# A three-stage token-mixing kernel: the first sequence's chain on two engines, another order at the mixer's beginning, and residuals loaded with the last chunk

## The chip, the cores and the metric

The kernel runs on one core of one Trainium2 chip. The core has a matrix engine (TensorE, PE in the profile), three engines for elementwise work (VectorE or DVE, ScalarE or ACT, GpSimd or POOL), and a SyncE queue (SP) that issues transfers; transfers run on 16 DMA engines. In this kernel matmuls read tiles in SBUF and write tiles in PSUM, from where DVE or ACT take them on. The metric is the device time of one execution in microseconds, as the median of several runs.

## The reference

The input x has 8 sequences of 1024 tokens with 128 channels (an image of 32 by 32). Two layers are computed, all in float32. Cut to what matters here:

```python
x = x + attention(group_norm(x))            # 4 heads of 32, q and k scaled to length 1, softmax over 1024 tokens
t = to_tokens(x)
t = t + mamba(layer_norm(t), forward weights) + reversed(mamba(reversed(layer_norm(t)), backward weights))
t = t + spectral_filter(layer_norm(t))      # 16 long filters over the sequence, by a Fourier transform
return t
```

In mamba the tokens are projected, a part of the projection passes a causal convolution of four taps per channel and a SiLU, a recurrence over chunks of 64 tokens follows, and its output is gated, normalised and projected back. The spectral filter transforms each sequence, multiplies every frequency by a 128 x 128 matrix and transforms back; the result is added to the residual t.

## The kernel before

One function, `fast_kernel`, holds all stages. In nearly all of them PE, DVE, ACT and POOL run their instructions in the order in which the program writes them (`manual_schedule(engines=IN_ORDER)`); in the mixer SP does too (`ALL_IN_ORDER`). Elsewhere a planner sets SP's order, and in the tail (L1589 to L1632) that of every engine.

**Attention (L591 to L816).** `qkv(b)` is a generator that makes q, k and v of one sequence, in steps divided by `yield`. PE transposes x (L609) into a PSUM tile `pt`. DVE copies it to the SBUF tile `xt` (L611) and takes statistics of `xt` (L615, L617). Two matmuls with one column each sum them over the groups of four channels; DVE works with small tiles between them (L622 to L630), and POOL computes the inverse root (L130, L132, tile names `gn_v` and `gn`). DVE normalises `xt` in place (L633). Then, for q and for k: two matmuls into `pq`, a DVE copy to SBUF (L648), and the squares' sum on ACT (L652). After the squares of q, POOL adds the output bias to x (L654). After those of k, POOL computes the inverse lengths (L656, L658), and DVE scales k by them (L673); between the two v is made (L662, L670). The scores need the scaled k.

`transforms` is another generator. It makes Fourier tables on DVE: for each table, angles (L289), then a rounding (L295, L297) and a clamp (L298); ACT turns them into sines (L302). The driver advances the generators by hand: for the first sequence in ten steps (L764 to L770), with one step of `transforms` behind each of the steps 1, 2, 3, 4, 5 and 7. Two steps of `qkv(1)` follow, and then 128 units of scores. PSUM tiles with the tag "t", the score tiles among them, come from a pool of three. `weighted` turns each half sequence's denominators over (copy, four reciprocals, two reductions, a product with `av`); for the last half this is finished in the mixer's beginning.

**Mixer (L826 to L1406).** Units are pairs of sequence and direction. A unit's steps are functions that the program calls in an order written out by hand:
- `project_x(u, n)` makes one half of the convolution's input on PE (`pp`, L935), `copy_x` copies it to SBUF on ACT (L955), `first_tap` writes one tap with the bias on ACT (L960), and `convolve` adds three taps on DVE (L968). `activate_x` is the SiLU.
- `add_decays` (`pdec`, L864 and L866), `turn_decays` and `take_decays` make tables of decays: small matmuls, ACT copies and exponentials, a store of `cums` to memory, and four loads that spread it over the tiles `lm` and `ec` (L889, L896). `from_row` is POOL's subtraction on `lm` (L912).
- `project_bc` is the matmul group `pb` (L990), `activate_bc` its SiLU (L1006).
- `project(B - 1, 1, ...)` (L427, L429) ends attention: four matmuls on `av` into `last_py`, and a DVE addition to x.

Wide PSUM tiles `w` come from `ps_w`, a pool of two.

**Filter chunks (L1485 to L1587).** 16 chunks of 8 frequencies. `matrices` combines the matrices of the next chunk (L1500) from `mst` into the tile `gs` (two buffers), `apply` multiplies (L1534) with the loaded spectra `u`, and `gather` sums (L1549 to L1555) and stores to `yd` (L1557). `fetch` reads the first part of `yd` back into `early_yt` (L1565).

**Tail (L1589 to L1632).** Four pieces (k, h): block of tokens and half of the sequences. `loaded` reads the piece's rows of `yd` into `yt` (two loads of 1 MB; the first piece has `early_yt`) and the residual from `xa` into `res` (1 MB). Three pieces are loaded ahead. `back` combines on DVE (`z`, L1608), transforms back on PE (`pz`, L1613), scales and adds to `res` on DVE (L1620), and stores 1 MB from ACT's queue (L1623).

Of the kernel before, what the change touches and what calls it, by code (L numbers as in the profile page):

```python
# [8 lines left out]
F32 = mybir.dt.float32  # L9
# [5 lines left out]
P = 128  # L15
B = 8
# [29 lines left out]
def fast_kernel(ctx: ExitStack, tc: tile.TileContext, a: dict, out: bass.AP, bad: bass.AP):  # L46
# [544 lines left out]
    with ExitStack() as s:  # L591
# [11 lines left out]

        def qkv(b):
# [6 lines left out]
            nc.vector.tensor_copy(xt, pt)  # L611
            yield
            st = p2.tile([P, 2, 6], F32, tag="st", name=f"st{b}")
            for i in range(2):
                nc.vector.bn_stats(st[:, i, :], xt[:, i * 512 : (i + 1) * 512])  # L615
# [21 lines left out]
            for i, (name, dst) in enumerate((("q", qs), ("k", ks))):  # L637
# [14 lines left out]
                nc.scalar.activation(junk, to, AF.Square, accum_out=ss[:, i : i + 1])  # L652
                if i == 0:
                    nc.gpsimd.tensor_tensor(xin, xin, bout.unsqueeze(1).to_broadcast([P, NT, C]), ALU.add)  # L654
                    yield
# [15 lines left out]
            vs.append(v)  # L671
            yield
# [91 lines left out]
        for at in range(10):  # L764
            next(coming)
            if at in (1, 2, 3, 4, 5, 7):
                next(making)
            if at == 4:
                sines(inv)
        next(coming, None)  # L770
        coming = qkv(1)
# [54 lines left out]
    with ExitStack() as s:  # L826
# [400 lines left out]
        def take_x(u, n):  # L1227
            project_x(u, n)
            copy_x(u, n)
            first_tap(u, n)  # L1230

# [13 lines left out]

        add_decays(first)
        turn_decays(first)
        take_decays(first)
        for _ in ending:
            pass  # L1250
        for n in range(2):
            take_x(first, n)
        add_decays(units[1])
        convolve(first, 0)
        activate_x(first, 0)
        project(B - 1, 1, av, wide_psum(ps_w, "last_py")[:, :512].rearrange("p (i c) -> p i c", i=4))
# [157 lines left out]
    with ExitStack() as s:  # L1414
        mp = s.enter_context(tc.tile_pool(name="c_m", bufs=1, side="right"))
        mst = mp.tile([P, 32, C], F32, name="mst")
# [68 lines left out]
        with ExitStack() as s2:  # L1485
# [103 lines left out]
        with ExitStack() as s2:  # L1589
            p2 = s2.enter_context(tc.tile_pool(name="i_2", bufs=2))  # L1590
            p3 = s2.enter_context(tc.tile_pool(name="i_3", bufs=3))
            ps_o = s2.enter_context(tc.tile_pool(name="i_ps_o", bufs=4, space=PSUM))

            def loaded(k, h):

                yt = early_yt
                if k or h:
                    yt = p2.tile([P, 2, 4, 4, C], F32, tag="yt", name=f"yt{k}_{h}")
                    for i in range(2):
                        nc.sync.dma_start(yt[:, i], yd[:, k, h * 4 : h * 4 + 4, i])  # L1600
                res = p3.tile([P, 4, 4, C], F32, tag="res", name=f"res{k}_{h}")
                nc.sync.dma_start(res, xa[h * 4 : h * 4 + 4, :, NB - 1 - k].rearrange("b p r c -> p b (r c)"))
                return yt, res

            def back(k, h, yt, res):
                z = p2.tile([P, 2, 2, 4, C], F32, tag="z", name=f"z{k}_{h}")
# [3 lines left out]
                for r in (0, 2, 1, 3):  # L1610
                    po = ps_o.tile([P, 4, C], F32, tag="o", name=f"pz{k}_{h}_{r}")
                    for i in range(2):
                        nc.tensor.matmul(  # L1613
                            po,
                            lhsT=inv[:, r, i, :],
                            rhs=z[:, r // 2, i] if r % 2 else yt[:, i, :, r // 2, :],
                            start=(i == 0),
                            stop=(i == 1),
                        )
                    nc.vector.scalar_tensor_tensor(  # L1620
                        res[:, :, r, :], po, keep[:, blk : blk + 1], res[:, :, r, :], ALU.mult, ALU.add
                    )
# [816 lines left out]
```

## Time and profile before

| What | us |
|---|---|
| median of 3 runs (lowest, highest) | 1432.75 (1431.81, 1436.02) |
| the profiled execution: its own time | 1432.01 |
| its span, first to last instruction | 1430.2 |
| 0 to 30: to the first scores, PE busy | 12.99 of 30.0 |
| 30 to 455.6: attention, PE busy | 418.29 of 425.6 |
| 455.6 to 481.6: the mixer's beginning, PE busy | 17.83 of 26.0 |
| 481.6 to 1026.9: mixer, PE busy | 513.83 of 545.3 |
| 1026.9 to 1116: filter, transforms, PE busy | 77.49 of 89.1 |
| 1116 to 1381.4: filter chunks, PE busy | 263.40 of 265.4 |
| 1381.4 to 1430.2: tail, PE busy | 30.89 of 48.8 |

Over the whole span PE is busy for 1334.7 us, DVE 1095.4, ACT 914.5 and POOL 529.5. In a timeline a line has the start, the duration, the engine, the line of the kernel, the operation, output and inputs, and in brackets the idle time of the engine before it and what ended that. "xN" joins N instructions in a row. A matmul of this kernel appears as two instructions. Busy time of PE includes modelled ends.

### The profile page before, as it was taken

Reading aid. Unit: us, or ns where it says so; the run is one execution under the profiler, and the core shown is the slowest. Engines: PE = TensorE matmul, PEld = TensorE weight load, DVE = VectorE, ACT = ScalarE, POOL = GpSimd, SP = SyncE. Lnnn points to the kernel's source line nnn. Section 1 sums busy time; section 2 is a strip of 40 time slices with the busy share of each in tenths; the row PEclk is TensorE's granted clock in tenths of the full one; section 3 lists DMA queues with packets and bytes.
Section 4 is the critical chain, followed back from the end, with each engine's and each line's share of the span. In section 5 each row is a group of like instructions: output and inputs, shape, how many; then the busy total and the mean of one; then the engine's idle time right before and its main releaser. Section 6 shows DMA issues by size and latency. Waiting matters only on the chain. (4 is left out here: it accounts for less than half of the span.)

```text
span 1430.2 us, 45285 instructions
## 1 busy us (share of the span) xinstructions
PE 1334.7 (93%) x19782; PEld 839.8 (59%) x19782; DVE 1095.4 (77%) x2138; ACT 914.5 (64%) x1421; POOL 529.5 (37%) x510
## 2 busy tenths in 40 slices
PE   5999999999998899999999999998799899999977
PEld 2323333233333566666666666666689899999963
DVE  5779888788768588979787988889644677777745
ACT  3665666766757678778787878786454555555520
POOL 3327866875610243324242424233476111111100
PEclk9999999999999899999999999999999999999989
DMA  7100111110000433434343444442459232222258
GB/s 182 40 1 21 55 38 38 38 51 25 8 1 19 102 76 79 100 90 105 75 105 88 94 92 114 95 106 46 132 190 232 73 89 76 71 77 70 72 153 324
DMA packets 139382, 123.09 MB, mean 86 GB/s; under 512 B 44808, under 2 KB 118152, under 8 KB 135080
## 3 DMA queue, kind: packets, MB, share of 16 engines
q1 hardware_dynamic: 137064, 115.93, 31.6%
q8 instruction: 157, 2.57, 0.8%
q10 hardware_dynamic: 2112, 4.19, 0.8%
q14 instruction: 49, 0.40, 0.1%
HBM read 78.15 MB, written 34.08 MB: 78 GB/s over the span
## 5 line engine op out<-in xcount | busy, mean ns | idle before, releaser
L696 ACT ACTIVATE pr<-pt 128x1024 f32<-128x1024 f32 x256 | 248.1, 1021 | 115.1 <-PE pt L691 113.5
L721 DVE TENSOR_TENSOR two<-pr,pr 128x1024 f32<-128x1024 f32 x128 | 162.9, 1313 | 20.5 <-ACT pr L696 19.6
L1513 ACT COPY gs<-pg 128x512 f32<-128x512 f32 x256 | 132.6, 602 | 64.4 <-PE pg L1500 47.9
L1511 DVE COPY gs<-pg 128x512 f32<-128x512 f32 x256 | 158.7, 682 | 15.3 <-PE pg L1500 9.6
L691 PE MATMUL pt<-q,k 32*128 32x512 f32 x1024 | 159.8, 654 | 7.0 <-ACT pr L696 4.7
L1500 PE MATMUL pg<-taps,mst 32*128 32x128 f32 x4096 | 146.0, 281 | 4.9 <-ACT gs L1513 4.1
L1500 PEld LDWEIGHTS pg<-taps,mst 32*128 32x128 f32 x4096 | 134.0, 189 | 17.1 <-issue 11.6
L712 PE MATMUL po<-pr,v 128*32 128x512 f32 x1024 | 139.9, 605 | 0.0
L926 POOL TENSOR_TENSOR ec<-ec,ct 128x2048 f32<-128x2048 f32 x16 | 83.4, 5212 | 135.3 <-ACT cums L868 59.2
L990 PE MATMUL pb<-bxt,wbc 128*128 128x512 f32 x256 | 116.9, 610 | 13.9 <-ACT zs L981 11.3
L1534 PE MATMUL py<-gs,u 128*32 128x128 f32 (+1 forms) x4096 | 127.8, 277 | 0.0
L968 DVE SCALAR_TENSOR_TENSOR xs<-xp,cw,xs 128x1024 f32<-128x1024 f32 x96 | 121.8, 1281 | 3.5 <-issue 1.7
L1534 PEld LDWEIGHTS py<-gs,u 128*32 128x32 f32 (+1 forms) x4096 | 112.0, 140 | 7.2
L1523 POOL TENSOR_SCALAR u<-u 128x512 f32<-128x512 f32 x16 | 24.0, 1498 | 229.3 <-PE pg L1500 128.5
L691 PEld LDWEIGHTS pt<-q,k 32*128 32x128 f32 x1024 | 47.6, 186 | 85.0 <-issue 32.2
L990 PEld LDWEIGHTS pb<-bxt,wbc 128*128 128x128 f32 x256 | 48.2, 193 | 73.1 <-issue 55.6
L1087 DVE SCALAR_TENSOR_TENSOR state<-state,dec,pst 128x64 f32<-128x64 f32 x448 | 87.3, 274 | 1.1
L1196 POOL TENSOR_TENSOR rms<-rms_v,mhalf 128x8 f32<-128x8 f32 x16 | 27.2, 1698 | 161.2 <-DVE rms_v L1194 161.2
L712 PEld LDWEIGHTS po<-pr,v 128*32 128x32 f32 x1024 | 27.8, 109 | 88.5 <-issue 84.6
L912 POOL TENSOR_TENSOR lm<-cs,lm 128x2048 f32<-128x2048 f32 x16 | 57.9, 3621 | 50.2 <-DVE xs L968 33.8
L732 PE MATMUL pd<-two,ones 128*32 128x512 f32 x512 | 73.0, 613 | 0.2
L1166 PEld LDWEIGHTS spo<-wo,y 128*128 128x128 f32 x512 | 62.1, 191 | 15.3 <-issue 10.3
(280 smaller groups left out, 2763.8 us busy)
## 6 DMA issues: line engine op xcount, KB each, us to landing
lm<-cd SPq DMA_DIRECT2D x32, 512.0 KB
ec<-cd SPq DMA_DIRECT2D x32, 512.0 KB
ud<-sp SPq DMA_DIRECT2D x8, 1024.0 KB
u<-ud SPq DMA_DIRECT2D x32, 256.0 KB
yd<-sums SPq DMA_DIRECT2D x32, 256.0 KB
moved<-state SPq DMA_DIRECT2D x48, 128.0 KB
yt<-yd SPq DMA_DIRECT2D x6, 1024.0 KB
X<-in_x SPq DMA_DIRECT2D x8, 512.0 KB
```

The lines of the kernel that those rows point to most:

```text
L691: nc.tensor.matmul(pt[:, i, :], lhsT=k[rows, j * P : (j + 1) * P], rhs=q[rows, cols], start=True, stop=True)
L696: nc.scalar.activation(pr[:, 2 * g : 2 * g + 2, :].rearrange("p i t -> p (i t)"), pt.rearrange("p i t -> p (i t)"), AF.Exp, scale=SCALE,)
L712: nc.tensor.matmul(po[rows, :], lhsT=vs[b][:, j, rows], rhs=pr[:, h, :], start=(j == 0), stop=(j == NT - 1))
L721: nc.vector.tensor_tensor(two, sums["pr"][:, 2 * g : 2 * g + 2, :], pr[:, 2 * g : 2 * g + 2, :], ALU.add)
L926: t = nc.gpsimd.tensor_tensor(u.ec, u.ec, u.ct.unsqueeze(1).to_broadcast([P, NH, NT, L]), ALU.mult)
L968: u.convolved = nc.vector.scalar_tensor_tensor(acc, xp[:, at : at + T], cw[u.d][:, n, i : i + 1], acc, ALU.mult, ALU.add)
L990: nc.tensor.matmul(u.pb[:, i * 512 : (i + 1) * 512], lhsT=wbc[u.d][:, k, :], rhs=xt[:, at : at + 512], start=(k == 0), stop=(k == KC - 1),)
L1087: nc.vector.scalar_tensor_tensor(u.state[:, k, h, :], u.state[:, k - 1, h, :], u.dec[:, c, h, j : j + 1], u.pst[c][:, j, h, :], ALU.mult, ...
L1500: nc.tensor.matmul(pts[g][:, e, :], lhsT=mst[rows, n * 4 + e, :], rhs=taps[rows, cols].rearrange("p f q m i -> p (f q m i)"), start=True, ...
L1511: nc.vector.tensor_copy(to, frm)
L1513: nc.scalar.copy(to, frm)
L1534: nc.tensor.matmul(py[t * 32 : t * 32 + 32 - 16 * m, q // 2, :], lhsT=u[:, i, m:, :, :, q * FC + f].rearrange("p k b i -> p (k b i)"), rhs ...
```

## The change

Three places change.

In attention, for the first sequence only: `xt` is copied by ACT, while DVE takes the statistics from PSUM; the squares are taken from PSUM (`pq`) instead of the SBUF copy; and the bias is added to x after v is made, not between q and k. The steps of `transforms` come later: three behind step 4, one each behind steps 5 and 7, and one after the end of `qkv(0)`.

In the mixer's beginning the first unit's `project_x` and `copy_x` for half 0 come first, then `add_decays`, the rest of `weighted`, and the other half. `turn_decays` and `take_decays` follow after that. `last_py` is made behind one tap of the convolution, and before the second unit's `add_decays`.

In the tail, residuals get two tiles that hold all pieces: `room`, a further buffer of the tag "gs", and a further buffer of the tag "mst". Of 4 MB, 3 MB are requested at the beginning of the last chunk, and 1 MB among the loads of `yt`. These lie in the rest of `room`, so that each piece has its own place. `z` takes buffers of the tag "u", `pz` those of the tag "g". The last piece is worked on in two halves of two sequences, each with its own store. The tail now lies within the block whose engines run in program order.

```diff
 def qkv(b):
...
-            nc.vector.tensor_copy(xt, pt)
+            first = b == 0
+            if first:
+                nc.scalar.copy(xt, pt)
+            else:
+                nc.vector.tensor_copy(xt, pt)
...
-                nc.vector.bn_stats(st[:, i, :], xt[:, i * 512 : (i + 1) * 512])
+                nc.vector.bn_stats(st[:, i, :], (pt if first else xt)[:, i * 512 : (i + 1) * 512])
...
-                nc.scalar.activation(junk, to, AF.Square, accum_out=ss[:, i : i + 1])
+                nc.scalar.activation(junk, pq if first else to, AF.Square, accum_out=ss[:, i : i + 1])
                 if i == 0:
-                    nc.gpsimd.tensor_tensor(xin, xin, bout.unsqueeze(1).to_broadcast([P, NT, C]), ALU.add)
+                    if not first:
+                        add_bias(xin)
                     yield
...
             vs.append(v)
+            if first:
+                add_bias(xin)
             yield
...
             next(coming)
-            if at in (1, 2, 3, 4, 5, 7):
+            for _ in range({4: 3, 5: 1, 7: 1}.get(at, 0)):
                 next(making)
             if at == 4:
                 sines(inv)
         next(coming, None)
+        next(making)
         coming = qkv(1)
...
+        project_x(first, 0)
+        copy_x(first, 0)
         add_decays(first)
+        for _ in ending:
+            pass
+        first_tap(first, 0)
+        project_x(first, 1)
+        copy_x(first, 1)
         turn_decays(first)
         take_decays(first)
-        for _ in ending:
-            pass
-        for n in range(2):
-            take_x(first, n)
+        first_tap(first, 1)
+        convolve(first, 0, range(1))
+        project(B - 1, 1, av, wide_psum(ps_w, "last_py")[:, :512].rearrange("p (i c) -> p i c", i=4))
         add_decays(units[1])
-        convolve(first, 0)
+        convolve(first, 0, range(1, pad))
         activate_x(first, 0)
-        project(B - 1, 1, av, wide_psum(ps_w, "last_py")[:, :512].rearrange("p (i c) -> p i c", i=4))
         convolve(first, 1)
...
+            def load_residuals(k, b, n):
+                nc.sync.dma_start(
+                    res[k][:, b : b + n].rearrange("p b r c -> p b (r c)"),
+                    xa[b : b + n, :, k].rearrange("b p r c -> p b (r c)"),
+                )
...
                 if c + 1 < chunks:
                     gs[c + 1] = p2.tile([P, P, C], F32, tag="gs", name=f"gs{c + 1}")
                     us[c + 1] = loaded_spectra(c + 1)
+                else:
+
+                    room = p2.tile([P, P, C], F32, tag="gs", name="room")
+                    res = [room[:, :32, :], mp.tile([P, 32, C], F32, tag="mst", name="res1")]
+                    res = [t.rearrange("p (b r) c -> p b r c", b=B) for t in res]
+                    load_residuals(1, 0, B)
+                    load_residuals(0, 0, 4)
...
+            for n, (k, h) in enumerate(pieces[1:], 1):
+
+                yts.append(room[:, 32 * n : 32 * n + 32].rearrange("p (i b q) c -> p i b q c", i=2, b=4))
+                for i in range(2):
+                    nc.sync.dma_start(yts[n][:, i], yd[:, k, h * 4 : h * 4 + 4, i])
+                if n == 2:
+                    load_residuals(0, 4, 4)
+            for yt, (k, h) in zip(yts, pieces):
+                z = p2.tile([P, 2, 2, 4, C], F32, tag="u", name=f"z{k}_{h}")
...
+                size = 2 if (k, h) == pieces[-1] else 4
+                for b in range(0, 4, size):
+                    bs = slice(b, b + size)
+                    to = res[blk][:, h * 4 + b : h * 4 + b + size]
+                    for r in (0, 2, 1, 3):
+                        po = ps_g.tile([P, 4, C], F32, tag="g", name=f"pz{k}_{h}_{b}_{r}")[:, :size]
...
+                        nc.vector.scalar_tensor_tensor(
+                            to[:, :, r, :], po, keep[:, blk : blk + 1], to[:, :, r, :], ALU.mult, ALU.add
+                        )
+                    nc.scalar.dma_start(
...
```

More of the change, by code (lines that the diff above doesn't have):

```diff
@@ L602, in fast_kernel, with add_bias @@
         qs, ks, vs = [], [], []
+        def add_bias(xin):
+            nc.gpsimd.tensor_tensor(xin, xin, bout.unsqueeze(1).to_broadcast([P, NT, C]), ALU.add)
         def qkv(b):
@@ L1225, in fast_kernel @@
         first, norms, av = units[0], {}, avs[1]
[L1227 to L1230, printed above, removed]
         def end(u, pool, waiting=None):
@@ L1415, in fast_kernel @@
         mp = s.enter_context(tc.tile_pool(name="c_m", bufs=1, side="right"))
-        mst = mp.tile([P, 32, C], F32, name="mst")
+        mst = mp.tile([P, 32, C], F32, tag="mst", name="mst")
         early_yt = mp.tile([P, 2, 4, 4, C], F32, name="early_yt")
@@ L1587, in fast_kernel @@
             fetch(chunks - 1)
[L1589 to L1606, printed above, removed]
+            pieces = [(k, h) for k in range(NB) for h in range(2)]
+            yts = [early_yt]
+            for n, (k, h) in enumerate(pieces[1:], 1):
[6 more added lines that the diff above has]
+                z = p2.tile([P, 2, 2, 4, C], F32, tag="u", name=f"z{k}_{h}")
                 for r, i, op in ((0, 0, ALU.subtract), (0, 1, ALU.add), (1, 0, ALU.add), (1, 1, ALU.subtract)):
@@ L1609, in back @@
                 blk = NB - 1 - k
[L1610 to L1618, printed above, removed]
-                        )
-                    nc.vector.scalar_tensor_tensor(
-                        res[:, :, r, :], po, keep[:, blk : blk + 1], res[:, :, r, :], ALU.mult, ALU.add
-                    )
@@ L1623, in back @@
-                nc.scalar.dma_start(
-                    out[h * 4 : h * 4 + 4, blk * 512 : (blk + 1) * 512].rearrange("b (p r) c -> p b (r c)", r=4), res
-                )
-            pieces = [(k, h) for k in range(NB) for h in range(2)]
-            got = [loaded(*piece) for piece in pieces[:3]]
-            for n, piece in enumerate(pieces):
-                back(*piece, *got[n])
-                if n + 3 < len(pieces):
-                    got.append(loaded(*pieces[n + 3]))
+                size = 2 if (k, h) == pieces[-1] else 4
@@ new lines, in fast_kernel @@
+                for b in range(0, 4, size):
[3 more added lines that the diff above has]
+                        po = ps_g.tile([P, 4, C], F32, tag="g", name=f"pz{k}_{h}_{b}_{r}")[:, :size]
+                        for i in range(2):
+                            nc.tensor.matmul(
+                                po,
+                                lhsT=inv[:, r, i, :],
+                                rhs=z[:, r // 2, i, bs] if r % 2 else yt[:, i, bs, r // 2, :],
+                                start=(i == 0),
+                                stop=(i == 1),
+                            )
+                        nc.vector.scalar_tensor_tensor(
+                            to[:, :, r, :], po, keep[:, blk : blk + 1], to[:, :, r, :], ALU.mult, ALU.add
+                        )
+                    nc.scalar.dma_start(
+                        out[h * 4 + b : h * 4 + b + size, blk * 512 : (blk + 1) * 512].rearrange(
+                            "b (p r) c -> p b (r c)", r=4
+                        ),
+                        to.rearrange("p b r c -> p b (r c)"),
+                    )
```

## The prediction

> **What bounds the kernel now.** I read the page's slices first, then the chain of waits, then the timelines of the three places that the diff touches, then TensorE's (PE's) granted clock there. From 30 us on PE is the busy engine of every stage: 418.3 of 425.6 us in attention (30 to 455.6), 513.8 of 545.3 in the mixer after its beginning, 263.4 of 265.4 in the filter chunks. The diff changes none of these loops. It works in the seams, where PE waits: 0 to 30 us (busy 13.0 of 30), 455.6 to 481.6 (17.8 of 26) and 1381.4 to the end (30.9 of 48.8). A microsecond taken from the waiting there is one off the end, as all later work hangs on it.
>
> The timeline of the first sequence (start, duration, engine, line; in brackets the idle time before and its releaser):
>
> ```profile
> 7.28 1.22 DVE L611 COPY xnt<-xt 128x1024 f32<-128x1024 f32 x1
> 8.53 1.29 DVE L615 BATCH_NORM_STATS2 st<-xnt 128x6 f32<-128x512 f32 x2
> ...
> 12.58 1.09 POOL L130 TENSOR_SCALAR gn_v<-var 128x1 f32<-128x1 f32 x1 [5.01 <-DVE var L630]
> ...
> 14.76 2.34 POOL L654 TENSOR_TENSOR X<-X,bout 128x1024 f32<-128x1024 f32 x1
> 14.82 2.83 DVE L633 TENSOR_SCALAR xnt<-xnt,mean,gn 128x1024 f32<-128x1024 f32 x1 [0.47 <-POOL gn L132]
> ...
> 25.55 1.06 ACT L652 ACTIVATE junkk<-k 128x1024 f32<-128x1024 f32 x1 [1.60 <-DVE k L648]
> ...
> 28.23 0.81 DVE L673 TENSOR_SCALAR k<-k,inv 128x1024 f32<-128x1024 f32 x1 [0.92 <-POOL inv L658]
> ```
>
> It is one chain on DVE, POOL and PE; PE's first scores start at 29.19, behind L673. See L633: 2.83 us where its median over eight is 0.76, beside the bias add on POOL.
>
> The mixer's beginning, PE and ACT:
>
> ```profile
> 464.27 1.16 PE L427 MATMUL last_py<-wout,av 128*128 128x128 f32 x8 [0.43 <-ACT xp L955]
> 467.99 10.05 PE L990 MATMUL pb<-bxt,wbc 128*128 128x512 f32 x16 [2.57 <-DVE X L429]
> ```
> ```profile
> 478.08 1.38 ACT L1006 ACTIVATE bt<-pb,cb 64x512 f32<-64x512 f32 x2 [5.21 <-PE pb L990]
> ```
>
> PE waits 2.57 us for one DVE addition (it frees pb's PSUM room), which stands behind three taps of 3.92 us; then the same 16 matmuls take 10.05 us that take 7.14 and 7.11 in the next two units. The stretches show why (us; busy time and count of PE, granted clock, DMA share, GB/s):
>
> ```profile
> 463.80:467.20 3.40, 1.20 (x9) 0.98 1.06 224
> 467.30:473.70 6.40, 5.71 (x7) 0.50 0.70 150
> 473.80:478.10 4.30, 4.24 (x10) 0.99 0.00 0
> ```
>
> The tail, from the chain of waits (start, us, what):
>
> ```profile
> 1381.41 0.32 SPq L1557
> ...
> 1381.84 7.56 DMA res<-xa
> ...
> 1389.59 10.04 PE pz L1613 x16
> ...
> 1400.57 9.38 DMA out<-res
> ...
> 1409.97 10.46 DMA res<-xa
> ```
> and from its timeline:
> ```profile
> 1383.65 0.64 SPq L1565 DMA_DIRECT2D early_yt<-yd  x2
> ...
> 1416.65 1.98 PE L1613 MATMUL pz<-yt,inv 128*128 128x512 f32 x4 [1.57 <-DMA yt<-yd]
> ...
> 1423.28 0.38 ACTq L1623 DMA_DIRECT2D out<-res  x1
> ```
>
> PE's first tail matmul needs only early_yt; its last 128 KB are issued at 1383.65 behind a 1 MB residual load and used at 1389.59. From 1390 to 1420 the DMA share is 1.03 to 1.06 at 380 to 410 GB/s: transfers set the tail.
>
> [...] L633 ends 0.55 us after POOL's addition (17.65 against 17.10). [...]
>
> **Start.** (a) The copy of xt goes to ACT, free then (a 1024-wide PSUM copy there: 0.99), and the statistics read PSUM at 7.28 instead of 8.53: 1.25 saved. PSUM reading can cost 0 to 0.1 (two 512-wide DVE copies from PSUM take 0.69 each); I take 0.1. (b) Table work moves behind the normalisation; the copy of the mean waited 0.3 for L289: saved. POOL's pair gn_v, gn took 2.2 beside DVE table work; its shortest instances are 0.19 and 0.58. Bounds 0.8 to 2.2; I take 1.0, so 1.2 saved. (c) L633 without the addition: 0.76, 2.07 saved. It ends 4.7 earlier (1.25-0.1+0.3+1.2+2.07), near 12.9. (d) Behind it DVE now has tables of 3.8 us (0.3+0.88+0.68+1.25+0.69); before, it waited 3.9 for pq there. The copy of q is not late. (e) The square of k reads PSUM when pk is done (6.55 after L633's end; ACT's sines and the square of q are over by 6.3), not after the DVE copy: 1.3 saved, so POOL's pair behind it starts 6.0 earlier. Copy of k, now behind the fwd angles, is 0.4 late but ends before that pair. (f) The bias add now stands directly behind this pair on POOL, as it stood before L633. L673 will be blocked as L633 was: 2.8 for 0.81, 2.0 given back. Bounds 0.8 and 2.9. (g) The last table step (1.22+0.69 on DVE) now stands before qkv(1)'s copy, which frees the third score tile for PE; ACT has exponentials for part of it: 0 to 1.9 lost, I take 1.0. Sum: 6.0-2.0-1.0 = 3.0 (1.0 to 6.0).
>
> **Mixer.** pp0 goes first and needs no POOL table: after pd at 455.6 instead of 459.0. By durations of the profile (pp 1.86 each, pdec group 1.35, ACT copy 1.0, tap 1.24): pp0 to 457.5, pdec to 458.9, pp1 to 460.8, its copy to 461.8. The denominators are ready at 461.7 as before (DVE's queue is unchanged up to there). last_py runs 462.0 to 463.2, the first tap on DVE 461.7 to 463.0, the freeing addition 463.2 to 463.95; pdec of the next unit ends on PE at 464.6; pb starts 464.6, not 467.99: 3.4. The work of PE between 455.6 and 464.6 leaves no gap over 1.3 us, so the clock should stay full and pb take 7.1, not 10.05: 2.9 more (bounds 0 and 2.9). pb's end, 471.7, meets ACT's second silu: DVE's taps end at 470.3 (461.7+six of 1.3+0.7), silu 471.4. The decays' store is issued 2.4 later (after 462.0), so the table lm, whose transfers ran 462 to about 467, lands near 470; POOL's L912 wants it only behind the taps. ACT's decay exponentials, with the second first tap behind them, and SP's five issues, behind which nothing waits, are thus covered; without this cover each us late would count. Sum 6.3 (3.4 to 6.4).
>
> **Tail.** 3 of 4 MB of residuals are to be loaded when the last chunk's matmuls free the two buffers (about 1371 and 1373): at 400 GB/s, 8 us, over near 1381 to 1383, beside 8.97 us of PE work that needs no DMA. On the SP queue, whose order is not written by hand here, the late yd stores and early_yt stand behind them. yd's last store comes at 1381.4 when most is over; early_yt then lands about 1387: PE starts 2.6 earlier (bounds -1 and 3.5). The 1.57 us stall and 0.4 of the 1.30 us wait for the last residual go: 7.4 MB (6.3 yt, 1 residual) need 19 us from 1386, and the last piece starts 24 us later. Last piece in halves: the same PE passes (128-wide ones run at 0.11, so 256-wide should scale), 0.3 lost to z; last addition 0.75 to about 0.42; last store 512 KB instead of 1 MB, whose transfer kept the DMA engines busy from 1424 to 1427: 1.4. One more store on ACT's queue costs nothing, ACT being idle. Sum 2.6+1.6+0.4-0.3+0.3+1.4 = 6.0 (2.4 to 7.5).
>
> **Total.** 3.0+6.3+6.0 = 15.3. The profiled execution took 1432.0 (span 1430.2 and 1.8 around): 1416.7. The median of three is 0.7 higher; I put the forecast between: 1417.0.
>
> **Rivals.**
> 1. Half clock stays for pb: 2.9 less gained, 1419.9. [...] against: PE's density.
> 2. The loads delay the read-back: SP waits in order for a yd store that lies behind 3 MB, PE starts at 1389.6 or later; with 3 less, 1420. For: one queue; against: the load fits into the last chunk.
> 3. L673 is not blocked: 2.0 more, 1415.0. For: DVE's table steps could shift the meeting; against: the same order gave the block at 14.8.
> 4. Slower: attention settles into another rhythm. Place: 128 score units of 3.3 us (425.6/128), three score tiles in turn; (g) shifts DVE against ACT at the first. Price: each 0.1 us per unit costs 12.6 over 126 units; from 0.09 the kernel is no longer measurably faster, and from 0.16 it is slower: (15.3+4.3)/126. At 0.17, 1438. For: ACT idles 115 us before its exponentials; against: orders and durations in the loop are the same, and PE is 98% busy there.
>
> **How the numbers follow.** Forecast 0.45, rival 1 0.17, rival 2 0.19, rival 3 0.12, rival 4 0.07. 0.3% (4.3 us) is about what can be told from no change. All but rival 4 are faster; of its 0.07 I give 0.02 to within 0.3% and 0.05 to slower: 0.93, 0.02, 0.05. The range 1411 to 1423 takes in rivals 1 to 3, the ends of (b), (f), (g) and the tail's bounds; above lie rivals 1 and 2 together and rival 4.
>
> **What would show it.** Right: L673 near 22 us but lasting some 2.8; bt starting 16.2 us after attention's last pd ends, not 22.5; clock 1.0 throughout pb; pz starting 5.6 after the last sums instead of 8.2; no DMA wait among pz. Wrong: gn_v and gn still 2.2; pb at 10; early_yt later than 8 us after the sums; exponentials in attention at another mean spacing.

## The result, and the profile after

The changed kernel takes 1418.7 us (median of four runs, 1414.25 to 1422.47) where the kernel before took 1434.17 beside it (four runs). The ratio is 0.9892, with an interval of 0.9857 to 0.9927: 1.1% less time. A second comparison, with five runs, gave 1418.27 and a ratio of 0.9907 (0.9892 to 0.9923). The prediction was 1417.0.

The profile after was taken in the shortest of the four runs (1414.25, span 1412.4). Its mean granted clock was 0.987; in the three other runs it was 0.978 to 0.981, as in the kernel before (0.978). Some of the difference between the two traces is therefore clock. The table cuts the span at marks that all kernels have. "Again" is the profile of the second comparison, with a clock of 0.979; "best" is the kernel that is put together at the end of the experiments.

| us | before | after | again | best |
|---|---|---|---|---|
| start to the first scores | 29.19 | 26.78 | 26.84 | 22.90 |
| to the end of attention's last pd | 426.41 | 424.49 | 427.15 | 426.63 |
| to the start of the second pb | 45.37 | 38.26 | 38.33 | 38.10 |
| to the end of the last pg | 870.19 | 867.29 | 869.91 | 869.05 |
| the last chunk's py, behind it | 8.93 | 10.61 | 11.81 | 11.81 |
| to the first pz | 9.50 | 7.36 | 7.53 | 7.46 |
| to the end | 40.61 | 37.61 | 37.13 | 38.15 |
| span | 1430.2 | 1412.4 | 1418.7 | 1414.1 |

Against "again", the start gives 2.4 us, the mixer's beginning 7.0, and the tail 2.6 (5.5 less 2.9 in py). The long loops between differ by under 1 us there. In the profile after they are 1.9 and 2.9 us shorter, which goes with its higher clock.

The start of the kernel after, from its timeline (start, duration, engine, line, operation; in brackets the idle time before it and what ended that):

```profile
8.09 1.30 DVE L623 BATCH_NORM_STATS2 st<-xt 128x6 f32<-128x512 f32 x2 [0.73 <-ACT xnt L617]
...
12.79 0.81 DVE L641 TENSOR_SCALAR xnt<-xnt,mean,gn 128x1024 f32<-128x1024 f32 x1 [0.97 <-POOL gn L132]
...
21.54 1.03 ACT L660 ACTIVATE junkk<-pk 128x1024 f32<-128x1024 f32 x1 [1.68 <-DVE k L656]
...
23.75 2.34 POOL L605 TENSOR_TENSOR X<-X,bout 128x1024 f32<-128x1024 f32 x1
...
23.82 2.82 DVE L684 TENSOR_SCALAR k<-k,inv 128x1024 f32<-128x1024 f32 x1 [1.77 <-POOL inv L667]
...
29.69 2.37 PE L702 MATMUL pt<-q,k 32*128 32x512 f32 x8 [0.81 <-DVE xnt L619]
```

See two waits between readers of one PSUM tile. The statistics wait 0.73 us for ACT's copy of the same `pt`. ACT, idle for 1.68 us, takes the square of k only when DVE's copy of the same `pk` is over; that is 1.4 us after the last matmul of `pk` (20.18). The bias addition on POOL now meets the scale of k, which takes 2.82 us as the normalise did before.

The mixer's beginning, from the timeline, and then from the stretches (us; busy time and count of PE, its weight loads, DVE, ACT, POOL; granted clock, DMA share, GB/s):

```profile
457.51 1.13 PE L427 MATMUL last_py<-wout,av 128*128 128x128 f32 x8 [1.01 <-ACT cs L889]
...
459.60 8.81 PE L1002 MATMUL pb<-bxt,wbc 128*128 128x512 f32 x16
...
468.45 1.38 ACT L1018 ACTIVATE bt<-pb,cb 64x512 f32<-64x512 f32 x2 [1.64 <-PE pb L1002]
```
```profile
455.50:459.60 4.10, 3.09 (x20) 1.94 (x18) 3.98 (x6) 3.37 (x8) 0.00 (x0) 1.00 0.04 8
459.60:463.00 3.40, 3.40 (x6) 1.42 (x6) 3.36 (x3) 2.73 (x4) 0.00 (x0) 0.51 0.77 164
463.00:468.40 5.40, 5.40 (x13) 2.09 (x11) 2.99 (x7) 1.06 (x1) 1.51 (x1) 0.99 1.02 215
```

From the end of pd (451.27) to pb there are 8.33 us instead of 12.39, and pb no longer waits for an addition. Here the granted clock was 0.51 for the first 3.4 us of pb, and the group took 8.81 us. In "again" it took 7.12, 1.7 less:

```profile
462.31 7.12 PE L1002 MATMUL pb<-bxt,wbc 128*128 128x512 f32 x16
```

In "again" a half-clock stretch of 6.8 us begins behind pb, at 472.0 (ten matmuls of sx took 2.40 us there, and 16 took 1.97 in the profile after), so that from pd to the second pb it takes 38.3 us in both.

The tail: the timeline of PE first, then the end of the chain of waits (start, us, what).

```profile
1356.76 8.33 PE L1546 MATMUL py<-gs,u 128*32 128x128 f32 x292
1366.30 1.13 PE L1546 MATMUL py<-gs,u 128*32 128x128 f32 x28 [1.22 <-issue]
1374.79 5.20 PE L1637 MATMUL pz<-early_yt,inv 128*128 128x512 f32 x8 [7.35 <-DMA early_yt<-yd]
...
1399.44 0.92 PE L1637 MATMUL pz<-room,inv 128*128 128x256 f32 x3 [1.85 <-DMA room<-yd]
```
```profile
1356.83 8.26 PE py L1546 x289
1368.73 2.39 DMA yd<-sums
1374.29 2.93 SPq L1580
1377.26 2.70 SPq L1621
1380.00 19.39 DMA room<-yd
1399.44 6.80 PE pz L1637 x30
```

The read-back is earlier, as wanted, but PE now stands idle inside the last chunk for 1.22 us, put down to "issue", that is, to nothing that the profile shows. Before, the chunk's matmuls ran without a gap:

```profile
1371.09 9.00 PE L1534 MATMUL py<-gs,u 128*32 128x128 f32 x320
```

In the tail behind it, a spectrum of 1 MB lands late: its load takes 19.39 us on the chain, and PE waits 1.85 us for it in the last of the four pieces.

### The profile page after: what moved, and what is told of

Its sections match the earlier page's. It is cut to its first block, busy times and chain, and to the rows that moved or that the text cites. A ratio compares the mean times of both kernels' runs of the same rounds, so it can differ in the third digit from the quotient of the medians.

```text
span 1412.4 us, 45313 instructions
## 1 busy us (share of the span) xinstructions
PE 1325.0 (94%) x19798; PEld 836.2 (59%) x19798; DVE 1093.9 (77%) x2141; ACT 916.0 (65%) x1423; POOL 530.2 (38%) x510
## 3 DMA queue, kind: packets, MB, share of 16 engines
q8 instruction: 157, 2.57, 0.8%
## 5 line engine op out<-in xcount | busy, mean ns | idle before, releaser
L1512 PEld LDWEIGHTS pg<-taps,mst 32*128 32x128 f32 x4096 | 133.8, 190 | 16.2 <-issue 11.4
L1178 PEld LDWEIGHTS spo<-wo,y 128*128 128x128 f32 x512 | 62.2, 192 | 15.3 <-issue 10.2
```

Source lines behind the costliest of these rows:

```text
L1512: nc.tensor.matmul(pts[g][:, e, :], lhsT=mst[rows, n * 4 + e, :], rhs=taps[rows, cols].rearrange("p f q m i -> p (f q m i)"), start=True, ...
```

## The experiments

**The three parts alone.** Each kernel is the kernel before with one part of the change; "again" is the whole. All four ran on one chip, beside 44 runs of the kernel before (1432.0).

```diff
 only_start: the edits in qkv and in the steps of transforms
 only_mixer: the other order of project_x to convolve
 only_tail: load_residuals, room, and the tail inside the ordered block
```

> The kernel before with the start's part alone. Theory 1 (the three parts add up[...]): first scores at 26.8 us instead of 29.2, L684 at 2.8 us again, median 2.5 us less than before (1 to 4). Rival (the start's gain is made up again in attention, and the 4.3 us seen at its end are the clock's): attention's last pd ends where it did before, 455.6, or within 1 us of it, once half-clock stretches in attention are counted. The second readers of a PSUM tile wait here as in the full change: statistics at 8.1 us behind ACT's copy, the squares of k behind DVE's copy.

> The kernel before with the mixer's part alone. Theory 1: from the end of attention's last pd to the second unit's pb group 38.3 us as in the full change, against 45.4 before: 7.1 less; the whole 7 us faster (5 to 8). Rival (what the reordering gains is only the wait of 3.4, the rest was a full clock by luck): 3.4 us, and the first pb group at 10 us.

> The kernel before with the tail's part alone. Theory 1: from the last pg to the end 3.5 us less than before (59.0 to 55.5), with a PE gap of over 1 us inside the last chunk's multiplications again while the residual transfers run, and the wait of about 1.9 us in the last piece. Rival (the gap in the last chunk was an accident of one run): no gap, last chunk 9.0 us as before, and 5 us less in all.

> The full change once more, as a measure of what changes from run to run. Theory 1: the parts outside of the diff differ from the first trace by whole or half stretches at half clock (1.7 us each), the three places by less than 1 us: first scores 26.8, pd to the second pb 38 to 40, last pg to the end 55 to 57. Rival (the clock follows from the order of the instructions): the half-clock stretches lie at the same work as in the first trace.

| | us | ratio (interval) |
|---|---|---|
| start alone | 1430.34 | 0.9984 (0.9974, 0.9994) |
| mixer alone | 1426.50 | 0.9965 (0.9953, 0.9977) |
| tail alone | 1430.15 | 0.9984 (0.9973, 0.9995) |
| whole | 1418.27 | 0.9907 (0.9892, 0.9923) |

All three parts gain, and the mixer's most. The mixer's gain shows in every trace: from pd to the second pb it takes 38.4 us in the kernel with the mixer part alone, 38.3 in "again", and 44.4 and 45.6 in the kernels without it. (Over all traces it is 36.6 to 38.4 in the eleven with the new order, and 44.4 to 45.6 in the three with the old one.) pb took 7.12 us in both kernels of this batch with the new order, so the long pb of the profile after is not set by this order. With the old order it took 8.65 and 10.17 in this batch, and 10.05 before.

The rival of the repeated run holds in part. All 14 traces have half-clock stretches at the same work: around the first scores, near 270 us, near 1025 and 1105, and in the tail. How long they are in sum differs (40.1 us in the profile after, 52.0 to 68.9 in the others), and so does whether pb has one; the profile before has two more, of 3.4 us at 108.7 and of 6.8 us at 480.7. By the clock records of the profiles before and after, each stretch lasted 3.4, 6.8 or 10.2 us, but for the one that runs to the end of the trace.

The start alone brings the first scores to 26.81 us. But in the two other kernels with the old start they stood at 28.03 and 27.98, not at 29.19: in the profile before, the four matmuls of pk took 2.89 us instead of 1.88. This goes with the clock: the trace's first record of full clock is at 23.32 us there, inside pk, and at 20.98 and 20.88 in the two others, ahead of it. Against these two the start's gain is 1.2 us. With the new start a fast pk does not help, as DVE's copy of it stands behind the tables' angles. The lines are from the kernel before, the mixer alone, and "again":

```profile
21.30 2.89 PE L640 MATMUL pk<-xnt,wqkv 128*128 128x512 f32 x4
```
```profile
21.14 1.88 PE L640 MATMUL pk<-xnt,wqkv 128*128 128x512 f32 x4
```
```profile
17.33 2.23 PE L648 MATMUL pk<-xnt,wqkv 128*128 128x512 f32 x4
...
18.72 1.65 DVE L289 TENSOR_SCALAR fwd<-odd,place 128x128 f32<-128x128 f32 x8
20.28 1.22 DVE L656 COPY k<-pk 128x1024 f32<-128x1024 f32 x1
```

In "again" pk is done at 19.56, but its copy starts no earlier than in the profile after (20.22).

The product of the three ratios is 0.9933, or 9.6 us; the whole is 13.3. Added as independent errors, the half widths of the four intervals come to some 3.5 us, beside a difference of 3.7. Whether the parts help each other stays open.

In the kernel with the tail alone, the last chunk's py took 12.40 us (8.93 before), with PE idle before its last 28 matmuls as in the profile after. So the gap comes with the tail's part. From the last pg to the end it takes 57.7 us there (59.0 before), and not the 55.5 expected: py is 1.8 us longer than in the profile after.

**Who waits at a PSUM tile.** The program's order of the two readers is turned round.

```diff
-            if first:
-                nc.scalar.copy(xt, pt)
-            else:
+            if not first:
                 nc.vector.tensor_copy(xt, pt)
...
                 nc.vector.bn_stats(...)
+            if first:
+                nc.scalar.copy(xt, pt)
...
+                if first:
+                    nc.scalar.activation(junk, pq, AF.Square, ...)
                 nc.vector.tensor_copy(to, pq)
```

> Kernel after, with the program's order of the two readers of a PSUM tile turned round in the first sequence: VectorE's statistics stand ahead of ScalarE's copy of xt, and ScalarE's squares of q and k stand ahead of VectorE's copies of q and k. Theory A (of two engines that read the same PSUM tile, the one that is later in the program waits for the other): bn_stats starts at 7.0 to 7.3 us in place of 8.09 with no idle time before it, ScalarE's copy starts only when the statistics end (8.4), the normalise starts near 12.0 in place of 12.79; the square of k starts when pk is done, some 1.3 us ahead of where it stood relative to pk, and VectorE's copy of k waits for it; the scale of k starts near 21.9 (before 23.82), the first scores near 25. Theory B (the statistics waited for the transposes or for ScalarE for another reason, such as its table load): bn_stats stays at 8.0 or later and the first scores stay within 0.3 us of 26.8. In time, A gives 1.5 to 2 us less than the kernel after, B no difference.

Measured: 1418.54 us, ratio 0.9903 (0.9884 to 0.9922). Its timeline:

```profile
7.28 1.29 DVE L621 BATCH_NORM_STATS2 st<-xt 128x6 f32<-128x512 f32 x2
...
18.93 1.03 ACT L658 ACTIVATE junkk<-pk 128x1024 f32<-128x1024 f32 x1 [0.21 <-PE pk L648]
...
19.89 3.83 DVE L289 TENSOR_SCALAR fwd<-odd,place 128x128 f32<-128x128 f32 x8
...
21.31 2.33 POOL L605 TENSOR_TENSOR X<-X,bout 128x1024 f32<-128x1024 f32 x1
...
23.65 1.21 DVE L659 COPY k<-pk 128x1024 f32<-128x1024 f32 x1
...
25.38 0.80 DVE L687 TENSOR_SCALAR k<-k,inv 128x1024 f32<-128x1024 f32 x1
```

It went as theory A has it: the statistics start at 7.28 without a wait (8.09 after a wait of 0.73 us in the profile after), and the square of k follows pk's end (0.21 us of idle time, for 1.68 in the profile after). So of two readers of these tiles the later one in the program's order waited for the other; what makes it wait is not shown. The prediction had counted on the two reads side by side. But the first scores came at 26.33, not near 25. Everything moved earlier, and POOL's addition now met DVE's table step (3.83 us for eight angles that took 1.65 in the profile after) ahead of the copy of k. So the addition slowed what DVE had beside it in three orders: the normalise before (2.83 us for 0.76), the scale of k after (2.82 for 0.81), and the angles here. Moving the chain only changed the victim, and the time did not fall by the 1.5 to 2 us of theory A.

**The bias addition out of the way.** POOL's addition moves from behind the inverse lengths into the attention loop.

```diff
-            if first:
-                add_bias(xin)
...
+            if n == 6:
+                add_bias(X[0])
```

> Kernel after, with GpSimd's addition of bout to the first sequence moved from behind the pair of small GpSimd operations to the seventh unit of the attention loop. Theory A (the addition of 2.34 us stretches VectorE's scale of k from 0.81 to 2.82 us): the scale of k takes 0.8 us, the first scores start at 24.8 in place of 26.8; then the third group of scores waits longer for VectorE's copy of the second sequence's xt, as the copy moves up by 2.0 us too. Theory B (the scale of k is long whatever GpSimd does, for instance by its scalars or by ScalarE's table load at 23.58): it stays at 2.8 us and the first scores at 26.8. In time, A gives up to 2.0 us less than the kernel after, B nothing.

Measured: 1417.15 us, ratio 0.9888 (0.9870 to 0.9906). From its timeline:

```profile
23.66 0.81 DVE L682 TENSOR_SCALAR k<-k,inv 128x1024 f32<-128x1024 f32 x1 [1.77 <-POOL inv L667]
...
24.62 2.09 PE L700 MATMUL pt<-q,k 32*128 32x512 f32 x8 [3.08 <-DVE k L682]
...
27.53 2.36 PE L700 MATMUL pt<-q,k 32*128 32x512 f32 x8 [0.81 <-DVE xnt L619]
```

Theory A: the scale takes 0.81 us and the scores start 2.2 us earlier. The third group of scores waits 0.81 us as before; its wait did not grow, since the copy before it moved by the same 2.2. The gain stands in the trace; the interval of the whole time overlaps with those of the kernel after.

**The order of the tail's loads.** The last megabyte of residuals is requested behind all spectra.

```diff
-                if n == 2:
+                if n == 3:
                     load_residuals(0, 4, 4)
```

> Kernel after, with the last megabyte of residuals requested behind the spectrum of the fifth piece (piece 4) in place of ahead of it. Theory A (piece 4's stall of 1.85 us comes from the queue's order): the stall in piece 4 before its last matmuls goes, the additions of pieces 4 to 7 start at once, and from the end of the last chunk's py to the end of the span it takes 43.2 to 43.6 us in place of 45.0. Theory B (what is late is the queue's bandwidth for 4 MB as a whole): the stall only moves to piece 2 or 3, whose additions want the last residuals, or to piece 5, and the time stays within 0.4 us.

(The expectation miscounts the pieces: there are four, and the stall is in the last.) Measured: 1419.28 us, ratio 0.9899 (0.9880 to 0.9918). From PE's timeline:

```profile
1398.94 3.60 PE L1637 MATMUL pz<-z,inv 128*128 128x512 f32 x8
1402.38 1.89 PE L1637 MATMUL pz<-room,inv 128*128 128x256 f32 x8
1404.11 2.39 PE L1637 MATMUL pz<-z,inv 128*128 128x256 f32 x8
```

The stall is gone, but the order of the loads need not be the reason. In "again", with the order of the kernel after, there is no stall either:

```profile
1381.57 6.26 PE L1637 MATMUL pz<-early_yt,inv 128*128 128x512 f32 x8 [7.54 <-DMA early_yt<-yd]
...
1404.83 1.89 PE L1637 MATMUL pz<-room,inv 128*128 128x256 f32 x8
```

In both traces the first eight pz took 6.45 and 6.26 us, against 5.20 in the profile after, where the half clock ended among them, at 1377.9; that it lasted longer in the two is the author's reading. So PE came later to the last piece and found its spectrum there. From the end of py to the end of the span it takes 45.8 us, against 45.0 in the profile after and 44.7 in "again". From 1375 to 1402 the kernel after moves 10.24 MB at a mean of 379 GB/s, at a DMA share of 1.01, so the DMA engines are full for those 27 us. Another order of the same loads gains nothing measurable; what it would do at full clock, and so theory A, stays open.

**Why PE stands idle in the last chunk.** The queue list of the profile has a kind "instruction" beside the data. This is the list of the kernel after over its whole span (packets, MB, share of 16 engines):

```profile
q1 hardware_dynamic: 137048, 115.93, 32.1%
...
q8 instruction: 157, 2.57, 0.8%
```

q8 moves packets of 16 KB (2.57 MB by 157). The profile after counts 19798 matmuls and as many weight loads, 126 of each for one packet. By the start times in the traces before and after, 128 matmuls start between one packet of q8 and the next (the median, in both). That q8 brings PE's instructions, 128 matmuls to a packet, is the author's estimate from these counts. With matmuls of py at 28 ns each (9.00 us by 320), 128 of them last 3.6 us. The same list for stretches of 0.5 us shows when a packet of q8 moved in the last chunk. Before, it is in those from 1372.0, 1376.0 and 1379.5. After, it is in those from 1357.5 and 1364.0. By the packets' own start times in the trace they are 3.7 us apart before (1372.34, 1376.09, 1379.78) and 6.2 us after (1357.89, 1364.07), so that the second packet comes some 2.5 us late, while residuals move at 390 GB/s and a DMA share of 1.04 (1360.5 to 1367.5). The late packet itself takes 0.98 us, where the median of q8 is 1.09: it starts late, and does not move slowly. It ends at 1365.04, and PE goes on 1.26 us later.

Four kernels try this. The first loads the residuals into the tile that the last chunk still reads. The second requests them behind the last `fetch`. The third makes three requests of 1 MB. The fourth holds them with a write on DVE.

```diff
 late_loads
-                    load_residuals(1, 0, B)
-                    load_residuals(0, 0, 4)
...
+                    early_room = p2.tile([P, P, C], F32, tag="gs", ...)
...
+            room = p2.tile([P, P, C], F32, tag="gs", name="room")
+            load_residuals(1, 0, B)
+            load_residuals(0, 0, 4)
 loads_behind
-                    load_residuals(1, 0, B)
-                    load_residuals(0, 0, 4)
...
             fetch(chunks - 1)
+            load_residuals(1, 0, B)
+            load_residuals(0, 0, 4)
 spread_loads
-                    load_residuals(1, 0, B)
-                    load_residuals(0, 0, 4)
+                    load_residuals(1, 0, 4)
...
                         gather(c, half, turn, py)
+                        if c == chunks - 1 and n < 2:
+                            load_residuals(1 - n, 4 - 4 * n, 4)
 loads_held (on the kernel "best" of the next experiment)
-                    load_residuals(1, 0, B)
-                    load_residuals(0, 0, 4)
...
             fetch(chunks - 1)
+            for k, b in ((1, 0), (0, 0), (0, 4)):
+                nc.vector.memset(res[k][:, b, 0, 0:1], 0.0)
+            load_residuals(1, 0, B)
+            load_residuals(0, 0, 4)
```

> Kernel after, with the residuals loaded into the tile that comes free only when the last chunk's matmuls have ended, and the spectra of the pieces into the other one, so that no residuals move during the last chunk. Theory A (the three megabytes that move beside the last chunk hold up TensorE, perhaps by its instructions[...]): the last chunk's py takes 8.9 us again (last pg end to last py end) with no idle gap put down to issue, where the three kernels that load the residuals there took 10.6, 11.8 and 12.4; the tail behind it is then late by the residuals, by 3 us or more, since the 3 MB take some 8 us behind the chunk's end. Theory B (the gap comes from the clock or from ScalarE and VectorE gathering sums): py takes 10.6 us or more here too.

> Kernel after, with its first three megabytes of residuals requested behind the read-back of the last chunk's sums, so that nothing of them moves beside the last chunk. (The run before with the loads in the other tile didn't do this: its loads began when half of that tile was free, inside the chunk.) Theory A (TensorE ran dry in the last chunk because the 16 KB instruction transfers, which the profile's queue list shows on the same DMA engines, came late behind the residuals): the last chunk's py takes 8.9 to 9.0 us with no idle gap, and the instruction transfers in it lie 3.9 us apart again, where they lay 6.5 to 7 us apart. Theory B (the gap belongs to the tail's new code or to its place in the instruction stream, whatever moves): the gap of 1 to 2 us after the 292nd matmul stays. In the tail behind it the first additions wait for residuals that share the DMA engines with 11 MB more: the whole is 2 to 6 us slower than the kernel after.

> Kernel after, with the same three megabytes of residuals in the last chunk in three requests of one megabyte: at its start, behind the first and behind the second store of sums. Theory A (what delays the instruction transfer is the backlog of up to three megabytes that stands before it on each DMA engine): the idle gap falls to 0.5 us or less, py takes 9.5 us or less, and the kernel is 1 us faster than the kernel after. Theory C (it is the share of the engines while they are full, whatever stands in the queue): the gap stays at 1 us or more and py at 10 us or more, and the time is the same within 1 us.

> The kernel of the best start, with its residual loads held back until the last chunk is done: a write of one column into each of the three parts, put on VectorE behind the last sums, stands ahead of each load, so that none of the 4 MB moves beside the last chunk (the two runs before that were to do this didn't, as the queue's order was made anew and the loads moved forward). Theory A (the instruction transfers come late behind the residuals, and TensorE runs dry): the last chunk's py takes 8.9 to 9.0 us with no idle gap put down to issue, and the instruction transfers in it lie some 3.9 us apart, in place of 6.5 to 7.5. Theory B (the gap belongs to this code's place in the instruction stream): the gap of 1 to 2.3 us after the 292nd matmul stays. Behind the chunk, the first additions wait for 2 MB requested ahead of the last read-back: the first pz starts up to 5 us later after the last sums, and the kernel is 1 to 6 us slower than that of the best start (1413.4).

| | us | ratio (interval) | last py | q8 seen in the 0.5 us from |
|---|---|---|---|---|
| late_loads | 1419.18 | 0.9899 (0.9883, 0.9916) | 12.40 | 1360.0, 1367.0 |
| loads_behind | 1420.20 | 0.9920 (0.9894, 0.9947) | 13.09 | 1360.0, 1366.0, 1372.0 |
| spread_loads | 1418.33 | 0.9910 (0.9884, 0.9935) | 11.50 | 1361.0, 1368.0 |
| loads_held | 1423.17 | 0.9930 (0.9904, 0.9955) | 8.94 | 1358.0, 1362.0, 1366.0 |

The first two did not do what they were made for. SP's order is made anew by the planner there, and both kernels issued their loads inside the chunk: at 1361.33 and 1366.43 in the first, at 1362.76 and 1366.43 in the second. What they show is the gap again, and in the second twice. Its timeline:

```profile
1362.66 4.85 PE L1546 MATMUL py<-gs,u 128*32 128x128 f32 x164
1368.48 3.76 PE L1546 MATMUL py<-gs,u 128*32 128x128 f32 x128 [0.97 <-issue]
1374.69 1.13 PE L1546 MATMUL py<-gs,u 128*32 128x128 f32 x28 [2.46 <-issue]
```

The gaps stand behind the 164th and the 292nd matmul, 128 apart, as many as start between two packets of q8 in the median. The ten traces with loads beside the last chunk have twelve such gaps (0.30 to 2.46 us), all at these two places, and after each PE goes on 1.0 to 1.5 us behind the end of a packet of q8. The four traces without such loads have none. With the loads held, the same place has no gap:

```profile
1357.24 9.01 PE L1550 MATMUL py<-gs,u 128*32 128x128 f32 x320
```

The packets of q8 are then 3.8 us apart (1358.44, 1362.27, 1366.03). The kernel "best" has a gap of 2.31 us there, and differs only in where the residuals are requested and in three small writes on DVE. This is what theory A expected: beside the residuals a packet of q8 comes late and PE stops (gaps of 0.30 to 2.46 us), and with the loads held neither is seen. That PE had run out of instructions then is the author's reading; the traces show the late packets and the gaps. In spread_loads the gap stayed at 2.12 us. That speaks for theory C, full engines rather than what stands in the queue, but the planner put the first two of its three requests together (both issued from 1360.23 on), so this is not settled.

Holding the loads back costs more than it saves. The first pz waits 11.93 us for the residual, as its request stands ahead of the last read-back, and the last piece waits for spectra (0.82 and 3.09 us). From the end of pg to the end of the span it takes 63.4 us, against 57.4 in "best". By the ratios the kernel is 7.3 us slower than "best", more than the 1 to 6 expected.

**The two findings on the start together.** Statistics ahead of ACT's copy, as in the run on the PSUM readers; the square of k, but not that of q, ahead of DVE's copy; the bias in the seventh unit.

```diff
+                ahead = first and i == 1
+                if ahead:
+                    nc.scalar.activation(junk, pq, AF.Square, ...)
                 nc.vector.tensor_copy(to, pq)
...
+            if n == 6:
+                add_bias(X[0])
```

> Kernel after, with what the two experiments on the start showed put together: statistics ahead of ScalarE's copy of xt, the square of k ahead of VectorE's copy of k (that of q stays behind its copy), and the addition of bout in the seventh unit. From those runs: normalise at 12.0 us, pk done near 18.8, square of k at 19.2, its scale (0.8 us) at 21.9, first scores at 22.9 us in place of 26.8. If nothing behind it takes this up, the kernel takes 3.9 us less than the kernel after (1414.4 against 1418.3). Rival: attention's rhythm takes back part of it, as the third group of scores waits for VectorE's copy of the second sequence[...]: then 1 to 2 us less.

Measured: 1413.42 us (six runs, 1412.43 to 1416.05), ratio 0.9879 (0.9859 to 0.9899). On the same chip spread_loads, whose start is that of the kernel after, took 1418.33. From the timeline of "best":

```profile
20.20 1.22 DVE L660 COPY k<-pk 128x1024 f32<-128x1024 f32 x1 [0.76 <-ACT junkk L659]
...
21.95 0.81 DVE L686 TENSOR_SCALAR k<-k,inv 128x1024 f32<-128x1024 f32 x1
...
22.90 1.74 PE L704 MATMUL pt<-q,k 32*128 32x512 f32 x8 [1.91 <-DVE k L686]
...
25.80 2.09 PE L704 MATMUL pt<-q,k 32*128 32x512 f32 x8 [1.16 <-DVE xnt L617]
```

The scores start at 22.90 as worked out, 3.9 us ahead of the kernel after, and attention takes 426.6 us as in "again" (427.2). The start's gain goes through to the end. The interval of "best" overlaps with both intervals of the kernel after, with the narrower one a little (0.9899 and 0.9892), so the step between the two rests on the traces; that "best" takes 1.2% less than the kernel before is clear.

## Why the prediction was right, and where it was not

The time was right to 1.7 us, and the gain came from the three seams, but part of the hit is luck. The three terms sum to 12.0 us in "again" where 15.3 was said: the mixer gave more, the start and the tail less. The first comparison's difference of 15.5 us meets the 15.3, but its interval spans some 10 us, and the second comparison gives 13.3. The terms:

**Start: 3.0 said, 2.4 to the first scores in the trace, 1.2 against the other traces of the old start.** The 3.0 has (g) in it, which comes behind the first scores; counted to the first matmuls on v, the trace has 1.5 (31.98 for 33.47).
- (a), 1.15 for the statistics: 0.44 (they start at 8.09 instead of 8.53). The step that failed is the belief that DVE and ACT can read one PSUM tile side by side. swap_reads shows that this wait, of 0.73 us, goes with the program's order and can be had for nothing.
- (b), 1.5 for the mean's wait and POOL's pair: from the start of the statistics to the normalise it takes 4.70 us instead of 6.29, so 1.6. POOL's pair takes 0.19 and 0.58, its shortest.
- (c), 2.07: 2.02. (d): the tables lie behind the normalise. The copy of q does not wait for them; that of k does, see (e).
- (e), 1.3 for the square of k: nothing. From the end of the normalise to POOL's `ss` it takes 9.14 us in both kernels. It is the same failed belief as in (a): the square waits for DVE's copy of k, and this copy now waits for the angles. Against the two traces of the old start with a fast pk (8.0 and 7.9) it is a loss of 1.1 to 1.2. The 6.55 us that the prediction took from L633's end to the end of pk held a pk of 2.89 us, where 1.88 stands in the two. POOL's second pair was 0.4 shorter, which was not in the sum.
- (f), 2.0 given back: 2.01. late_bias shows the cause: with the addition elsewhere the scale took 0.81 us.
- (g), 1.0: a wait of 0.81 us in the third group of scores, where the old start shows none.

**Mixer: 6.3 said, 7.0 measured.** pb starts 4.1 us earlier after pd (8.3 for 12.4; 3.4 said) and takes 7.12 us instead of 10.05 (2.9 said). Rival 1, half clock for pb, did happen in the profile after, for one stretch of 3.4 us, but in none of the ten other profiles with this order: pb takes 7.12 us in each of them. In the three traces with the old order pb took 8.65 to 10.17. That the clock would stay full with no gap over 1.3 us was the author's estimate; the profile before shows for it only one stretch, with PE busy for 1.20 of the 3.40 us ahead of the half clock. In the profile after PE was busy for 3.09 of the 4.10 us ahead of it, so the estimate did not hold there; why this one run had the stretch is not shown.

**Tail: 6.0 said, 3.5 measured in the profile after and 2.6 in "again".** PE starts 2.1 us earlier after py (2.6 said). What failed is the sentence "beside 8.97 us of PE work that needs no DMA". That work stopped for 1.22 and 2.05 us, went on only after a packet of q8 had come, and took 10.61 and 11.81 us. This is 1.7 of the missing 2.5 in the one, and 2.9 of 3.4 in the other. The longer py takes the read-back's gain again: from the last pg to the first pz it takes 18.0 and 19.3 us, against 18.4 before. The stall of 1.57 did not surely go: the profile after has one of 1.85 in its place. "Again" has none, but took longer over the first eight pz, and from the first pz to the end both take much the same (37.6 and 37.1). The half-sized last store counted for less than 1.4 in most kernels: from the last addition's end to the end it takes 5.7 us after (6.95 before), but 6.5 in "best" and 6.9 in yt_first.

Rival 2, loads that delay the read-back in SP's queue, did not come about: behind py it is 2.1 us earlier. Rival 3 did not come about, as (f) held. Nor did rival 4: attention takes 427.2 us in "again", against 426.4 before, and (g)'s wait is in the 427.2.

Of the signs named for being right, the long scale of k came (at 23.82, not near 22). `bt` starts 17.2 us after pd in the profile after and 15.5 in the ten others of this order, where 16.2 was said. The first pz starts 6.1 us after the last sums, where 5.6 was said and 8.2 stood before. A DMA wait among the pz was to be absent, and the profile after has one.

What stays open: why the three parts alone sum to less than the whole, what the order of the tail's loads is worth, and how the delay of a packet of q8 depends on the queue ahead of it.

## What to carry to other kernels

Before two engines read one PSUM tile to save a copy, ask which of them stands first in the program, and put the one on the critical chain there (here the statistics then started at 7.28 us instead of 8.09). When a long operation on GpSimd must be moved, move it to where VectorE has nothing urgent for its whole length, not only to behind the instruction that it blocked (the scale of k took 2.82 us beside it, and 0.81 without it). And when transfers are to be hidden behind dense matmuls, look at the queue of the kind "instruction" too (here q8, 157 packets of 16 KB): the matmuls of the last chunk read only SBUF, and took 10.61 us beside 3 MB of residuals in the profile after and 8.93 without them before. No order of loads tried here avoided this at a profit.

## What the runs showed of the hardware that was not expected

- While the DMA engines moved 390 GB/s, a packet of 16 KB on q8 started 6.2 us after the one before it, where 3.7 us stood in the profile before. PE stopped beside such loads for 0.3 to 2.5 us, at places exactly 128 matmuls apart (3.6 us of matmuls at 28 ns each), and went on 1.0 to 1.5 us after a packet of q8 had come.
- The half-clock stretches lie at much the same work in all traces, but not each of them in each run: the same pb had one in the profile after, where 8.81 us were taken, and none in "again" (7.12). In the stretch before it PE was busy for 3.09 of 4.10 us. This stretch of 3.4 us cost pb 1.7 us, and a run has several (40.1 to 68.9 us in sum), so differences of 2 us between single traces mean little outside the place of an edit.
- The two reads of `pt`, `pq` and `pk` of the first sequence by ACT and DVE ran one after the other in all traces of kernels with the new start, in the order of the program. Where the second engine had no other work, it stood idle for 0.2 to 1.7 us before its read.
